# Order of a Strassen unit's products and of one closing product; deferred multiplications; later residual loads in an RWKV block with a feed-forward layer

## The chip, the cores and the metric

The kernel runs on one NeuronCore of a Trainium2 chip. The time is the device time of one execution in microseconds (us); of the kernel before there are three runs, and their median is the number that counts. The profile of a further execution gives the time of every instruction. Engines are named PE (TensorE matmuls), PEld (TensorE weight loads), DVE (VectorE), ACT (ScalarE), POOL (GpSimd) and SP (SyncE, which here only issues DMAs). PE, DVE and ACT each run their instructions in the order in which the program wrote them; they meet through semaphores. The order of the DMA issues on SP and POOL is set by the tile scheduler from the same program.

## The reference

The input is 2048 tokens of width 512 in float32. First comes an RWKV block on the normalised input, then a gated feed-forward layer:

```
y0 = layer_norm(x);  h = layer_norm(y0);  hh = time_shift(h)
k, v, r = (h*tm + hh*(1-tm)) @ W.T          (three mixes, three weights)
y  = y0 + sigmoid(r) * wkv(k, v) @ Wo.T
h  = layer_norm(y);  hh = time_shift(h)
kk = (h*cm_mk + hh*(1-cm_mk)) @ Wkey.T        (512 to 2048)
y  = y + sigmoid((h*cm_mr + hh*(1-cm_mr)) @ Wcr.T) * (silu(kk) @ Wval.T)
x  = x + y
z  = layer_norm(x)
out = x + (silu(z @ gate.T) * (z @ up.T)) @ down.T    (512 to 2048 to 512)
```

The wkv step needs only elementwise work per token. Nearly all the time is in the matrix products.

## The kernel before

**Blocks.** The tokens are worked off in four blocks of 512 (b = 0 to 3). The RWKV part of all blocks comes first, then the feed-forward part (FFN) of each block: for g = 0 to 3 a gate unit and an up unit (each 512 x 512 weights), then the down projection.

**A unit.** Each 512 x 512 x 512 product is split into quarters of 256 and done with Winograd's form of Strassen's scheme: seven products of quarters instead of eight. A1, A2, ... are quarters of the weights, B1, ... of the activations, S1 to S4 and T1 to T4 their sums. `unit` (L662 to L751) writes the seven products as steps. A product of quarters is 8 matmul records of 128x256. The steps share PSUM banks: an own bank z, and the two banks `accv` and `accx` that all units have in common.

- step 1 (A11 B11) fills z; ACT copies z to accv (L701).
- step 2 (A12 B21) adds on accv, which is then the output quarter (0,0) and goes to `sink`.
- step 6 (S2 T2) adds on z; ACT copies z to an SBUF tile u2 (L712).
- step 5 (S1 T1) adds on z; ACT copies z to accx (L716). DVE's `u2 -= accx` is put off by one product with `later` (L717).
- step 7 (S3 T3) adds on z: output quarter (1,1).
- step 3 (S4 B22) adds on accx: output quarter (0,1).
- step 4 (A22 T4) adds on z; DVE adds u2, which is output quarter (1,0).

Steps 7, 3 and 4 are not done at once: they go into the list `held`, and the next unit does them one at a time between its own steps (`pop_held`). So the common banks pass from one unit to the next while both are under way. The order of a unit of one weight is in L748; about 35 of 41 units find three held steps of a unit before them.

**Deferred work.** `later(fn, n)` puts a function on one list, `put_off`; each product calls `due()`, which counts the entries down and runs those that are due from the front of the list, in order. `tick` runs background work (mixes, norms, sums of weights) as far as a planner's estimate of DVE's time allows.

**Paired units.** In the FFN of blocks 1 to 3 the products A11 B11 and S3 T3 of a unit are themselves split once more (`inner`, L772 to L855); `paired_unit` (L859 to L946) works on banks accz, accw, accv and accx and adds the inner results (`pair`). Copies L930 and L931 bring an inner result into PSUM banks. Sinks of a gate unit apply Silu; those of an up unit multiply by the gate's result and write the hidden activations.

**Down projection.** `down_product` (L1615 to L1769) has seven outer products, each again split in seven on quarter-size tiles of 128x128 (one[0] to one[6]); z steps (0, 2, 4, 5, 6) add on one bank, and ACT copies it out after most of them (L1696); y steps (1, 3) add on another bank. `quads` are sums of the hidden activations.

**Loads.** Weights come through a ring of 12 tiles, issued by SP. `load_resid` (L1396) issues, on SP, one 1 MB load of the residual and four x loads of 256 KB; `paced` ties each to the end of the last product written before it. `ffn_in` adds them, takes the norm and transposes it into the next block's activations.

Of the kernel before, what the change touches and what calls it, by code (L numbers as in the profile page):

```python
# [64 lines left out]
def rwkv_ffn_kernel(  # L65
# [584 lines left out]
    held = []  # L650
# [11 lines left out]
    def unit(weights, Bs, sink, by_token, done=None, free=None):  # L662


        acc, tmp = {}, {}
        last = len(weights) - 1

        def product(z, a, b, first=False, between=None, part=None, read=None):
            if first:
                acc[z] = bank()  # L670
            pz = acc[z]
            groups = list(range(last + 1) if part is None else part)
            for g in groups:
                wg = weight(weights[g], a)
                act = Bs[g][b]
                for m in range(2):
                    for k in range(2):
                        lo = slice(m * P, (m + 1) * P)
                        lhsT = act[:, k, lo] if by_token else wg[:, k, lo]
                        rhs = wg[:, k, :] if by_token else act[:, k, :]  # L680
                        mm = nc.tensor.matmul(  # L681
                            pz[:, m, :],
                            lhsT=lhsT,
                            rhs=rhs,
                            start=first and g == 0 and m == 0 and k == 0,
                            stop=g == last and k == 1,
                            skip_group_check=True,
                        )
                latest[:] = [mm.ins.name]
                if read is not None and g == groups[-1]:  # L690
                    read()
                due()
                if g < groups[-1]:
                    tick()
                    if between is not None and g < 2:
                        between()

        def step1():
            acc["v"], acc["x"] = accv, accx
            product(  # L700
                "z", A11, B11, True, pop_held, read=lambda: nc.scalar.copy(accv, acc["z"])  # L701
            )

        def step2(part=None):
            product("v", A12, B21, part=part)
            if part is None or last in part:
                sink(0, 0, accv)

        def step6():
            product("z", S2, T2)  # L710
            tmp["u2"] = u_tile("u2")
            nc.scalar.copy(tmp["u2"], acc["z"])  # L712

        def step5():
            product("z", S1, T1)
            nc.scalar.copy(accx, acc["z"])  # L716
            later(lambda: tt(tmp["u2"], tmp["u2"], accx, ALU.subtract), 1)  # L717

        def step7():
            product("z", S3, T3)  # L720
            sink(1, 1, acc["z"])

        def step3():
            product("x", S4, B22)
            sink(0, 1, accx)

        def step4():
            product("z", A22, T4)
            tt(tmp["u2"], acc["z"], tmp["u2"], ALU.add)

            later(lambda: sink(1, 0, tmp["u2"]), 1)
            if free is not None:
                free()
            if done is not None:
                later(done, 2)
            quiet[0] = True

        if last > 0:

            def most():  # L740
                step2(range(last))

            def rest():
                step2([last])

            order = (step1, None, most, step6, rest, step5)
        else:
            order = (step1, None, step2, step6, None, step5, None)  # L748
        for s in order:
            if s is None:  # L750
                pop_held()  # L751
            else:
                s()
                tick()
        held.extend(((STEP, step7), (STEP, step3), (STEP, step4)))
# [103 lines left out]
    def paired_unit(at, b, n, after, sink, done=None, free=None):  # L859


        B = Lazy((b, "z"))
        st, steps = ahead.pop(at, (None, ()))
        for f in steps:
            f()
        steps = []
        if after is not None:
            ahead[after[0]] = inner(after[2], after[1])
            steps = ahead[after[0]][1]

        def small():
            if steps:
                steps.pop(0)()

        def product(dst, q, k, start=False):
            wg = weight(n, q)
            act = B[k]
            for m in range(2):
                for kk in range(2):
                    mm = nc.tensor.matmul(  # L880
                        dst[:, m, :],
                        lhsT=wg[:, kk, m * P : (m + 1) * P],
                        rhs=act[:, kk, :],
                        start=start and m == 0 and kk == 0,
                        stop=kk == 1,
                        skip_group_check=True,
                    )
            latest[:] = [mm.ins.name]
            due()

        z, aw = acc2["z"], acc2["w"]
        plus = None if st is None else st["r"][:, 1]
        u2 = None
        small()
        pop_held()
        if st is None:
            product(z, A11, B11, True)
            nc.scalar.copy(accv, z)
            tick()
            pop_held()  # L900
        small()
        product(z, S2, T2)
        if st is None:
            u2 = u_tile("u2")
            nc.scalar.copy(u2, z)
        else:
            nc.scalar.copy(aw, z)
        tick()
        pop_held()
        small()  # L910
        product(accv, A12, B21)
        sink(0, 0, accv)
        tick()
        if st is None:
            plus = bank()
            product(plus, S3, T3, True)
            tt(u2, plus, u2, ALU.add)
            plus7 = u_tile("p7")
            nc.scalar.copy(plus7, plus)
            plus = plus7  # L920
            tick()
        small()
        product(z, S1, T1)
        nc.scalar.copy(accx, z)
        sink(1, 1, z, plus)
        tick()
        small()
        if after is not None:
            r = ahead[after[0]][0]["r"][:, 0]
            nc.scalar.copy(z, r)  # L930
            nc.scalar.copy(accv, r)  # L931
        product(aw, A22, T4, st is None)
        end = sink(1, 0, aw, plus if u2 is None else u2)
        if end is not None:
            later(end, 1)
        tick()

        def last():
            product(accx, S4, B22)
            sink(0, 1, accx)  # L940
            if free is not None:
                free()
            if done is not None:
                later(done, 1)

        held.append((STEP, last))  # L946
# [509 lines left out]
    def ffn_gate(b, g):  # L1456
# [4 lines left out]
        def sink(i, j, c, plus=None):  # L1461
            t = tile_of("s")
            s[i, j] = t
            if plus is not None:
                tt(t, c, plus, ALU.add)
                c = t
                if (i, j) == (1, 0):
                    return lambda: nc.scalar.activation(t, t, AF.Silu)
            nc.scalar.activation(t, c, AF.Silu)

        if b == 0:
# [21 lines left out]
    def ffn_up(b, g):  # L1493
# [3 lines left out]
        def sink(i, j, c, plus=None):  # L1497
# [1 line left out]
            if q not in hid:  # L1499
                hid[q] = hidden_tile()  # L1500
            h = hid[q][:, g]
            if plus is not None:
                tt(h, c, plus, ALU.add)
                c = h
            tt(h, c, s[i, j], ALU.mult)
            if g == 3:
                made.add((b, q))
                if q in (B11, B22):
                    quarter_sums(b, 0 if q == B11 else 1)

        done = lambda: hidden_done(b, g)
        free = op_done if g == 3 else None
# [99 lines left out]
                parts.append(("T3", B22, B12))  # L1612
            urgent((b, "quarters", n, 1), run(parts))

    def down_product(b, sink, weight_of, final, done=None):  # L1615
        base = {}

        def summed(n, r):
# [49 lines left out]
        def steps(n):  # L1668
# [46 lines left out]
            def fifth():  # L1715
                product(st["z"], S1, T1, False)
                keep(0, 1)
                if n + 2 < 7:
                    later(lambda: quarter_sums(b, n + 2, (0,)), 1)
                later(rest, 1)  # L1720

            def rest():
                r = st["r"]
# [24 lines left out]
        for n in range(7):  # L1748
# [4 lines left out]
            one[0]()  # L1753
            tick(half)
            pop_held()
            one[1]()
            tick(half)
            if final and n == 6:
# [15 lines left out]
    def ffn_down(b):  # L1774
# [16 lines left out]
                store(1, cols)  # L1791
                store(0, slice(HB, HB + P))

        down_product(b, sink, down_weight, final)

# [81 lines left out]
    for b in range(NB):  # L1879
        for g in range(4):  # L1880
# [2 lines left out]
                ffn_gate(b, g)  # L1883
            if g == 1 and b == 0:
                push((b + 1, "z", "t"), ffn_in(b + 1), op_free)
            if g == 0 and 0 < b < NB - 1:
                load_resid(b + 1)
            ffn_up(b, g)
            if g == 0 and b == 0:
                load_resid(b + 1)  # L1890
            if g == 0 and 0 < b < NB - 1:
                push((b + 1, "z", "t"), ffn_in(b + 1), op_free)
        if b + 1 < NB:
            need((b + 1, "z"))
            ffn_gate(b + 1, 0)
# [83 lines left out]
```

## Time and profile before

| What | Value |
|---|---|
| Runs | 1229.54, 1229.62, 1232.41 us; median 1229.62 |
| Profiled execution | 1232.75 us, span from first to last instruction 1231.0 us |
| Mean granted TensorE clock | 0.998 |
| PE busy | 1216.0 us |
| DVE busy | 819.9 us |
| ACT busy | 408.1 us |
| POOL busy | 214.3 us |
| DMA | 321.98 MB, mean 262 GB/s |

A line of the timeline has the start in us, the duration, the engine, the line of the kernel, the operation, output <- inputs and the shape; the brackets at the end hold the engine's idle time before it and what ended it. In a list of waits the three numbers behind the colon are the total in us, the number of waits, and the longest. A wait of PE is written as what PE was about to do, an arrow, and the engine, tile and line that it waited for. A matmul group on the timeline that shows a wait also pays some 0.2 us until matmuls follow each other at the usual pitch of 0.22 us (128x256) or 0.11 us (128x128), so costs of stalls are best read from starts.

### The profile page before, as it was taken

How to read it: one execution, taken by the hardware profiler on the slowest of the kernel's cores; microseconds unless marked ns; L12 is line 12 of the kernel's file. 1: busy time of each engine (PE TensorE's matmuls, PEld its weight loads, DVE VectorE, ACT ScalarE, POOL GpSimd, SP SyncE). 2: the span in 40 equal slices, each digit the busy share in tenths (PEclk: the TensorE clock that was granted, in tenths of full speed). 3: DMA queues.
4: the chain of work that ended last, by engine and by line, in shares of the span. 5: the costliest groups of instructions: out<-in, count | busy, mean ns of one | idle time of the engine just before them, and what ended most of it. 6: DMA issues, size and time to landing. Idle time of an engine off the chain costs nothing.

```text
span 1231.0 us, 20030 instructions
## 1 busy us (share of the span) xinstructions
PE 1216.0 (99%) x7124; PEld 1106.3 (90%) x7124; DVE 819.9 (67%) x1530; ACT 408.1 (33%) x824; POOL 214.3 (17%) x386
## 2 busy tenths in 40 slices
PE   8999999999999999999999999999999999999998
PEld 7888888888888888998899888999999899999998
DVE  5886676677586667885867776557556575565466
ACT  5534252352532334313312222124431243323321
POOL 1332221223222223002205651000000000000000
PEclk9999999999999999999999999999999999999999
DMA  5768996799888989899889864896669856796576
GB/s 179 258 221 281 304 300 229 272 331 294 285 261 274 310 280 308 252 296 379 269 269 331 289 223 145 268 334 188 201 217 298 313 185 204 247 302 225 181 255 205
DMA packets 161978, 321.98 MB, mean 262 GB/s; under 512 B 19272, under 2 KB 32728, under 8 KB 160600
## 3 DMA queue, kind: packets, MB, share of 16 engines
q1 hardware_dynamic: 135312, 236.25, 59.5%
q0 software_dynamic: 24960, 81.81, 18.4%
q10 hardware_dynamic: 1608, 2.65, 0.6%
q8 instruction: 57, 0.93, 0.3%
q14 instruction: 41, 0.34, 0.1%
HBM read 267.15 MB, written 53.49 MB: 260 GB/s over the span
## 4 chain that ended last, share of the span: by engine, by line
PE 84%; DMA 6%; DVE 5%; ACT 2%; issue 2%; POOL 1%; ACTq 0%; POOLq 0%; DVEq 0%; SPq 0%
PE ps L681 26%; PE ps L1684 21%; PE accz L880 6%; PE accx L681 5%; PE accv L681 5%; PE ps L797 5%; PE ps L974 5%; PE accv L880 3%; PE accx L880 3%; PE accw L880 3%; PE ps L566 1%; DMA raw<-d 1%; DMA raw<-in_w 1%; DMA dd<-raw 1%; DMA raw<-in_wd 1%
## 5 line engine op out<-in xcount | busy, mean ns | idle before, releaser
L681 PE MATMUL ps<-mix,w 128*128 128x256 f32 x920 | 211.2, 379 | 1.7 <-ACT u L712 1.7
L681 PEld LDWEIGHTS ps<-mix,w 128*128 128x128 f32 x920 | 173.9, 190 | 25.6 <-ACT u L712 2.1
L1684 PE MATMUL ps<-w,hid 128*128 128x128 f32 x1248 | 156.9, 275 | 0.4 <-ACT r L1696 0.4
L1684 PEld LDWEIGHTS ps<-w,hid 128*128 128x128 f32 x1248 | 149.3, 192 | 1.4 <-ACT r L1696 0.5
L1684 PE MATMUL ps<-w,quads 128*128 128x128 f32 x1056 | 133.7, 275 | 0.9 <-ACT r L1696 0.7
L1684 PEld LDWEIGHTS ps<-w,quads 128*128 128x128 f32 x1056 | 126.1, 192 | 1.8 <-ACT r L1696 1.4
L1696 ACT COPY r<-ps 128x128 f32<-128x128 f32 x168 | 44.5, 266 | 205.6 <-PE ps L1684 202.4
L510 DVE TENSOR_TENSOR raw<-raw 128x512 f32<-128x512 f32 x92 | 63.3, 688 | 41.9 <-issue 18.6
L880 PE MATMUL accz<-zT,w 128*128 128x256 f32 x376 | 89.0, 380 | 0.0
L510 DVE TENSOR_TENSOR hid<-hid 128x512 f32<-128x512 f32 x126 | 86.2, 698 | 2.3
L880 PEld LDWEIGHTS accz<-zT,w 128*128 128x128 f32 x376 | 68.0, 190 | 7.4
L974 PE MATMUL ps<-mix,w 128*128 128x256 f32 x320 | 72.4, 386 | 1.1 <-DVE mix L518 1.1
L1780 POOL DMA_DIRECT2D out<-resid x12 | 8.6, 718 | 356.6 <-DVE resid L510 331.0
L974 PEld LDWEIGHTS ps<-mix,w 128*128 128x128 f32 x320 | 61.4, 194 | 10.2 <-DVE mix L518 1.8
L510 DVE TENSOR_TENSOR r<-ps,r 128x256 f32<-128x256 f32 x83 | 29.8, 359 | 57.9 <-PE ps L1684 53.6
L510 DVE TENSOR_TENSOR r<-r 128x128 f32<-128x128 f32 (+1 forms) x83 | 41.1, 496 | 36.3 <-ACT r L1696 34.9
L681 PE MATMUL ps<-w,t 128*128 128x256 f32 x264 | 59.4, 379 | 0.0
L510 DVE TENSOR_TENSOR quads<-hid,quads 128x512 f32<-128x512 f32 x84 | 57.7, 687 | 1.4
L797 PEld LDWEIGHTS ps<-inner,w 128*128 128x128 f32 x352 | 52.6, 191 | 6.2 <-ACT pair L808 1.5
L701 ACT COPY accv<-ps 128x512 f32<-128x512 f32 x41 | 23.4, 571 | 100.4 <-PE ps L681 97.6
L681 PEld LDWEIGHTS ps<-w,t 128*128 128x128 f32 x264 | 50.1, 190 | 6.8
L681 PE MATMUL ps<-zT,w 128*128 128x256 f32 x248 | 56.0, 379 | 0.0
(228 smaller groups left out, 2167.5 us busy)
## 6 DMA issues: line engine op xcount, KB each, us to landing
w<-in_w SPq DMA_DIRECT2D x237, 256.0 KB, 4.2
w<-sum SPq DMA_DIRECT2D x220, 256.0 KB, 4.1
w<-dd SPq DMA_DIRECT2D x112, 256.0 KB, 3.6
w<-vsum SPq DMA_DIRECT2D x56, 256.0 KB, 4.4
w<-vv SPq DMA_DIRECT2D x56, 256.0 KB, 3.9
w<-d SPq DMA_DIRECT2D x48, 256.0 KB, 3.6
w<-in SPq DMA_DIRECT2D x44, 256.0 KB, 3.6
q<-in_w POOLq DMA_DIRECT2D x36, 256.0 KB, 6.7
```

The source lines that it names most:

```text
L510: nc.vector.tensor_tensor(out, a, b, op)
L566: nc.tensor.transpose(flat[:, t * P : (t + 1) * P], h[:, t, c * P : (c + 1) * P], ident)
L681: mm = nc.tensor.matmul(pz[:, m, :], lhsT=lhsT, rhs=rhs, start=first and g == 0 and m == 0 and k == 0, stop=g == last and k == 1, skip_gro ...
L701: "z", A11, B11, True, pop_held, read=lambda: nc.scalar.copy(accv, acc["z"])
L797: m = nc.tensor.matmul(dst[:, i, :], lhsT=wt(i, q), rhs=act(i, k), start=start and i == 0, stop=True, skip_group_check=True,)
L880: mm = nc.tensor.matmul(dst[:, m, :], lhsT=wg[:, kk, m * P : (m + 1) * P], rhs=act[:, kk, :], start=start and m == 0 and kk == 0, stop=kk ...
L974: mm = nc.tensor.matmul(acc[i, j][:, m, :], lhsT=act[:, k, lo] if by_token else wg[:, k, lo], rhs=wg[:, k, :] if by_token else act[:, k, : ...
L1684: mm = nc.tensor.matmul(dst, lhsT=x[k][:, g, :], rhs=wt[:, g, :], start=first and g == 0, stop=g == 3, skip_group_check=True,)
L1696: nc.scalar.copy(st["r"][:, m, n * P : (n + 1) * P], st["z"])
L1780: eng.dma_start(out_t[b][:, tokens, cols], rs[b][:, tokens, cols])
```

## The change

There are four parts.

1. In `unit`, where three steps are held from a unit before, the order of a one-weight unit is step 1, held 7, held 3, step 6, step 2, held 4, step 5 instead of step 1, held 7, step 2, step 6, held 3, step 5, held 4. 
2. In paired units the second operation of the (1,1) and (1,0) sinks (Silu for gate, the multiplication for up) is put off by one product. Before, this was so for the gate's (1,0) only.
3. In the last of the seven outer products of block 0's down projection (n = 6, `alone`) the steps go 0, 2, 4, 1, 5, 3, 6 in one piece, with none held for what follows, and `rest` (the sums of r) is put off by three products instead of one.
4. For blocks 1 and 2 `load_resid(b+1)` is put off by four products into `ffn_up(b, 0)`; `ffn_in(b+1)` is pushed ahead of `ffn_up(b, 1)` instead of behind `ffn_up(b, 0)`.

```diff
@@ unit
             order = (step1, None, step2, step6, None, step5, None)
+            if len(held) == 3:
+                order = (step1, None, None, step6, step2, None, step5)
@@ paired_unit
-        sink(1, 1, z, plus)
+        later(sink(1, 1, z, plus), 1)
...
-        end = sink(1, 0, aw, plus if u2 is None else u2)
-        if end is not None:
-            later(end, 1)
+        later(sink(1, 0, aw, plus if u2 is None else u2), 1)
@@ ffn_gate, sink
                 tt(t, c, plus, ALU.add)
-                c = t
-                if (i, j) == (1, 0):
-                    return lambda: nc.scalar.activation(t, t, AF.Silu)
+                return lambda: nc.scalar.activation(t, t, AF.Silu)
@@ ffn_up, sink
-            if plus is not None:
-                tt(h, c, plus, ALU.add)
-                c = h
-            tt(h, c, s[i, j], ALU.mult)
-            if g == 3:
-                made.add((b, q))
-                if q in (B11, B22):
-                    quarter_sums(b, 0 if q == B11 else 1)
+
+            def end():
+                tt(h, c if plus is None else h, s[i, j], ALU.mult)
+                if g == 3:
+                    made.add((b, q))
+                    if q in (B11, B22):
+                        quarter_sums(b, 0 if q == B11 else 1)
+
+            if plus is None:
+                return end()
+            tt(h, c, plus, ALU.add)
+            return end
@@ down_product
-                later(rest, 1)
+                later(rest, 3 if alone and n == 6 else 1)
...
             pop_held()
+            if alone and n == 6:
+                one[2]()
+                tick(half)
+                pop_held()
+                for k in (4, 1, 5, 3, 6):
+                    one[k]()
+                    tick(half)
+                continue
             one[1]()
@@ ffn_down
-        down_product(b, sink, down_weight, final)
+        down_product(b, sink, down_weight, final, alone=b == 0)
@@ FFN loop
+            if g == 1 and 0 < b < NB - 1:
+                push((b + 1, "z", "t"), ffn_in(b + 1), op_free)
             if g == 0 and 0 < b < NB - 1:
-                load_resid(b + 1)
+                later(lambda: load_resid(b + 1), 4)
             ffn_up(b, g)
...
-            if g == 0 and 0 < b < NB - 1:
-                push((b + 1, "z", "t"), ffn_in(b + 1), op_free)
```

## The prediction

> **What bounds the kernel now.** I read the page first (busy time, then the chain that ended last), then PE's waits, then the timeline around each wait that the change can reach.
>
> ```profile
> PE 1216.0 (99%) x7124; PEld 1106.3 (90%) x7124; DVE 819.9 (67%) x1530; ACT 408.1 (33%) x824; POOL 214.3 (17%) x386
> ...
> PE 84%; DMA 6%; DVE 5%; ACT 2%; issue 2%; POOL 1%; ACTq 0%; POOLq 0%; DVEq 0%; SPq 0%
> ```
>
> PE is never idle for long, so time changes only where PE's waits come or go. The change adds and removes no matmul. PE's waits, with us in total, times and longest:
>
> ```profile
> PE ps L681 <- ACT u L712: 1.7, 1, 1.7
> PE accx L880 <- DMA w<-sum: 1.4, 1, 1.4
> ...
> PE ps L1684 <- ACT r L1696: 1.1, 3, 0.4
> ...
> PE accv L681 <- ACT accv L701: 0.9, 1, 0.9
> ...
> PE ps L797 <- ACT pair L808: 0.7, 2, 0.4
> ```
>
> These are all that the change can take away. By starts of successive matmuls, slow restart included, they cost 1.94 (at 426.67), 1.63 (973.32), 1.25 (813.71 and 815.22), 1.17 (321.10) and 1.24 (906.09 and 1048.41): 7.2 us.
>
> **1. The order in `unit` (about 35 of 41 units).** One product of 8 matmuls is 1.73 us. Before: s1, s7', s2, s6, s3', s5, s4' (a prime is a held step of the unit before). After: s1, s7', s3', s6, s2, s4', s5. ACT's copies get more room: accv's copy to s2 has three products instead of one, u2's copy to s5 two instead of one. So the 1.17 us at 321.10, a wait for the copy of accv, goes. What gets less room is s5's end: s5 copies its bank to accx, DVE then does `u2 -= accx`, and only then may s3 write accx. Before, five products lay between s5 and s3; now two do, 3.46 us. In the trace of before this DVE operation has enough room:
>
> ```profile
> L716 ACT COPY accx<-ps x41: 570/570/580, 109.0 to 764.5; 128x512 f32<-128x512 f32 x41
> ...
> DVE u L510: 28.1, 17
> ```
>
> The copy ends 0.55 to 0.76 us after s5. The subtraction ends 1.3 to 3.1 us after s5 in most units, which still fits, but +4.06 (at 109), +4.04 (214), +5.30 (315), +5.57 (415), +6.36 (583) and +5.37 (595) in six. With unchanged lags these six would stall 0.7 + 0.7 + 2.0 + 2.2 + 3.0 + 2.0 = 10.6 us against the 3.3 us that are free: one end. The other end is no stall at all and both old ones gone: -3.1. DVE's own order changes too, so I follow it unit by unit in the order of instructions that the change produces.
>
> The worst place is the r unit behind a k unit (blocks 2 and 3). The deferred list is served in order, and the k unit's last operation, due two products later, stands ahead of `u2 -= accx`; so DVE meets it only when s3 is next. This is what DVE does there in before:
>
> ```profile
> 254.91 0.69 DVE L518 SCALAR_TENSOR_TENSOR e<-e,r 128x512 f32<-128x512 f32 x1 [0.76 <-ACT r L1246]
> 255.51 0.68 DVE L510 TENSOR_TENSOR u<-u,accx 128x512 f32<-128x512 f32 x1
> 256.12 0.69 DVE L510 TENSOR_TENSOR u<-ps,u 128x512 f32<-128x512 f32 x1
> 256.73 0.68 DVE L510 TENSOR_TENSOR raw<-raw 128x512 f32<-128x512 f32 x1
> 257.33 0.61 DVE L514 TENSOR_SCALAR r<-u,nfirst 128x256 f32<-128x256 f32 x2
> 260.27 1.42 DVE L518 SCALAR_TENSOR_TENSOR mix<-hT_b,vec,mix 128x512 f32<-128x512 f32 x2 [2.33 <-ACT mix L619]
> 261.98 0.75 DVE L518 SCALAR_TENSOR_TENSOR mix<-hT_b,vec,mix 128x512 f32<-128x512 f32 x1 [0.29 <-ACT mix L619]
> ```
>
> The reader sees the subtraction at 255.51, ahead of the mix operations that wait for ACT. In after it is behind them. With the end of k's s4 as zero: u add to 0.9 and tensor_scalar to 1.5 (DVE), two Exp to 2.85, accx copy to 3.4, two mix activations to 4.7, accv copy to 5.3, one mix to 5.9 (ACT); DVE's third mix waits for that and ends at 6.7, the product with e at 7.4, the subtraction at 8.1. PE does s5 to 1.73, s1 to 3.46, s7 to 5.2, and s3 then waits until 8.2: 3.0 us. In block 3 the same chain holds, with raw loads that held DVE from 413.82 to 418.01 in before: 3.0 if they are in time, 6.0 if as late as then; I take 4.3, nearer to the first since the wait is shared, less the 1.94 us of 426.67 which these later copies replace: +2.4. At the value units near 585, with another raw load ahead, I take +1.2 (0 to 4). The other units keep 0.1 to 1.8 us of room. Sum 3.0 + 2.4 + 1.2 - 1.17 = **+5.4** (-3.1 to +10.6).
>
> A stall of this length would be new for this kernel; its longest in mid-run is 1.94 us, and the granted clock stays 0.998. The Trainium skill, "TensorE: Matmul & The Clock Gate", section "What's actually happening", says that TensorE drops to half clock after at least one idle window of about 3.4 us and needs another such window of work to come back. By that rule each of up to four new stalls could cost 1.7 us more (an estimate from that page), and the sum would be some 7 us higher. No row here has an idle time that long, and the sum goes without it.
>
> **2. Residual loads behind a unit's first weights (blocks 1 and 2).** `load_resid(b+1)` issues 1 MB of resid and four x loads of 256 KB. It is paced on a product that is now four products later, in the up unit's first product round. On SP these five go ahead of the S2 weight of the next gate unit; that weight stands behind them in the same queue. What this queue did at the place in before:
>
> ```profile
> 959.24 0.33 SPq L1398 DMA_DIRECT2D resid<-res  x1
> 959.78 2.65 SPq L310 DMA_DIRECT2D x<-in_x  x4
> 962.78 0.33 SPq L206 DMA_DIRECT2D w<-sum  x1
> 963.93 1.14 SPq L256 DMA_DIRECT2D w<-in  x2
> 967.31 1.00 SPq L206 DMA_DIRECT2D w<-sum  x2
> ```
>
> ```profile
> 973.32 1.53 PE L880 MATMUL accx<-zT,w 128*128 128x256 f32 x6 [1.40 <-DMA w<-sum]
> ```
>
> The weight issued at 967.31 had waited on the residual's landing and came 1.63 us late at 973.32. That stall goes. What is late next is the S2 weight. Between the pace point and the S2 product that reads it PE has 0.43 + 1.73 + 0.43 + 1.73 + 0.86 + 1.73 + 0.43 = 7.34 us of work. In block 1 of before resid was issued at 816.41, the weight behind x at 819.45, and it landed at 827.15: 10.7 us after resid's issue, itself 0.2 behind its pace point: 10.9, so 3.6 us too late. In block 2 the two weights issued next (963.93) landed 12.6 us after resid's issue, the one ahead of them (962.78) some 1.2 us earlier: 11.4, 4.1 too late. Together 7.7 less 1.63: **+6.1**. Lower bound: weights alone land 4.1 us after issue, which with 3.3 us of issue ahead is 7.4, no stall, hence -1.6. Upper: 5 us each, +8.4. I take the value near the top because the megabytes ahead are the same and move on the same queue. SP's later issues shift with it; POOL issues none of the moved loads. The adds and statistics of the next `ffn_in`, pushed one unit later, have DVE's idle third and a whole unit as cover; without it they would delay transposes, some 0.7 us each.
>
> **3. The closing product of block 0's down projection.** Two z steps in a row wait for ACT's copy of r:
>
> ```profile
> 813.71 1.16 PE L1684 MATMUL ps<-w,hid 128*128 128x128 f32 x8 [0.35 <-ACT r L1696]
> 815.22 1.05 PE L1684 MATMUL ps<-w,quads 128*128 128x128 f32 x7 [0.35 <-ACT r L1696]
> ```
>
> The new order 0, 2, 4, 1, 5, 3, 6 puts a y step between them, and the sums go to the end: -1.25. The first inner product then waits for the product's last addition, one DVE operation of 0.36 us of which about 0.2 shows: **-1.05** (-1.25 to +0.4).
>
> **4. Multiplications put off by a product in paired units.** The pair addition that ACT's copies L930 and L931 wait for came at 904.12, behind a 0.69 us multiplication. With this moved behind it, the addition starts up to 0.7 earlier, but its own product ends near 903.8. Two stalls of 0.62 shrink: **-0.8** (-1.24 to +0.3, if a gate's Silu, later by 1.7 us, holds up its multiplication).
>
> **Sum:** 5.4 + 6.1 - 1.05 - 0.8 = +9.6. The profiled execution took 1232.75 us (span 1231.0), 0.25% over the median of the runs, 1229.62. So 1242.4 for such an execution and 1239.2 on the median.
>
> **The rivals.** 0.3% (3.7 us) is what a measurement of this kernel can tell from no change.
> - *The room that is left suffices (faster).* The old stalls go, and what is late in my working arrives in time: `u2 -= accx` within 3.3 us of s5, the S2 weight within 7.34 us of the pace. For it: most lags are under 3.1 us, and a weight alone lands in 4.1. Against it: mix operations ahead of the subtraction, megabytes ahead of the weight. It gives -7.2 + 0.2: 1222.6. It decides as long as all new stalls together stay under 7.2 - 3.7 = 3.5 us; one late S2 weight uses that up.
> - *The load stalls come, the units are neutral.* If DVE's work in the r units is done earlier than I place it: 0 + 6.1 - 1.85 = +4.3: 1233.9.
> - *The unit stalls come, the loads don't.* 5.4 - 1.6 - 1.85 = +2: 1231.6, not distinguishable.
> - *Raw loads hold DVE in more units.* With the 10.6 end of part 1 and 5 us for each load: 10.6 + 8.4 - 1.85 = +17: 1246.8.
> - *Nothing visible.* The prolonged stalls are used up by others downstream: PE has no slack to give back, so this needs all terms small: 1229.6.
>
> **How the numbers follow.** My forecast 0.50; loads only 0.16 (slower, barely); raw loads 0.10; units only 0.09 and nothing 0.03 (same); all gains 0.12 (faster). Faster 0.12, same 0.13 with a little of the second case, slower 0.75. The range from 1228 to 1245 leaves out most of the gains case and half of the worst one. The likeliest case alone has 1235 to 1244.
>
> **What would show it.** In the changed profile PE's waits hold no ACT r L1696 pair and no accv L701; new entries are a wait of s3 (accx) for DVE u of about 3 us near 258 and again near 425, and two of the S2 product (accz) for DMA w<-sum of 3 to 4 us near 827 and 970. The prediction is wrong if the S2 weight overtakes the residual, if DVE reaches the subtraction before the mix operations, or if the clock falls behind a long stall.

## The result and the profile after

The changed kernel takes 1242.08 us (median of six runs, 1240.33 to 1244.87); the kernel before took 1231.06 us in its six. The ratio is 1.0091 with a 95% interval of 1.0073 to 1.0109, some 11 us slower. The profiled execution has a span of 1243.1 us, 12.1 more than before. It was also the longest of the six runs, so single sizes below are those of one execution.

The first line is the busy time on the page of the changed kernel; the others are PE's waits (us in total, times, longest).

```profile
PE 1221.1 (98%) x7124; PEld 1109.4 (89%) x7124; DVE 819.6 (66%) x1530; ACT 411.3 (33%) x824; POOL 214.9 (17%) x386
```

```profile
PE accz L882 <- DMA w<-sum: 4.6, 2, 3.1
PE accx L681 <- DVE u L510: 4.0, 3, 2.4
PE ps L681 <- ACT accx L716: 3.5, 3, 2.1
...
PE ps L1686 <- ACT r L1698: 0.4, 1, 0.4
```

The reader sees the exchange: all five old entries (ACT u, DMA w<-sum at accx, the pairs of ACT r and ACT pair, ACT accv) are gone, and three new ones have come. They are the three resources that the change gave less room: the S2 weight, `u2 -= accx`, and the copy to accx. PE's busy time rose by 5.1 us although it does the same 7124 matmuls; that is explained below.

By starts of matmuls (time over the usual pitch, restart included) the whole difference can be placed:

| Place in the changed kernel | before | after |
|---|---|---|
| 113, s3 waits for DVE u | 0.8 | 2.0 |
| 172.6, s7 waits for ACT accx | 0 | 0.7 |
| 222, transposes wait for DVE h | 0.3 | 1.25 |
| 264.65, s3 waits for DVE u | 0 | 2.7 |
| 321, s2 waits for ACT accv | 1.2 | 0 |
| 424 to 429 | 1.9 | 4.95 |
| 488.6, s7 waits for ACT accx | 0 | 1.2 |
| 515, 596, 763 | 1.1 | 0.3 |
| 813 to 827, closing product and after it | 1.7 | 0.7 |
| 841.8, S2 weight, block 1 | 0 | 1.8 |
| 985.3, S2 weight, block 2 | 0 | 6.1 |
| old late weight (973) | 1.6 | 0 |
| pairs (906, 1048) | 1.2 | 0 |

The differences add up to 11.9 of the 12.1 us: +7.8 up to 763 (the units, the transposes near 222 and the small waits at 515, 596 and 763), loads +6.3, closing product -1.0, pairs -1.2. Of the 2.0 at 113, 0.85 stands before and after alike, near 108.

The place behind the k unit, DVE's timeline of the changed kernel, answers to the lines shown of before:

```profile
258.32 0.69 DVE L510 TENSOR_TENSOR raw<-raw 128x512 f32<-128x512 f32 x1
260.90 1.42 DVE L518 SCALAR_TENSOR_TENSOR mix<-hT_b,vec,mix 128x512 f32<-128x512 f32 x2 [1.89 <-ACT mix L619]
262.64 0.75 DVE L518 SCALAR_TENSOR_TENSOR mix<-hT_b,vec,mix 128x512 f32<-128x512 f32 x1 [0.33 <-ACT mix L619]
263.31 0.69 DVE L518 SCALAR_TENSOR_TENSOR e<-e,r 128x512 f32<-128x512 f32 x1
263.92 0.68 DVE L510 TENSOR_TENSOR u<-u,accx 128x512 f32<-128x512 f32 x1
```

PE's timeline there:

```profile
255.13 7.13 PE L681 MATMUL ps<-mix,w 128*128 128x256 f32 x32
264.65 1.56 PE L681 MATMUL accx<-mix,w 128*128 128x256 f32 x6 [2.39 <-DVE u L510]
```

The subtraction now stands behind three mix operations, which wait for ACT (1.89 and 0.33 us), and behind the product with e, and s3 waits for it.

SP's timeline in block 2, then PE's:

```profile
974.82 0.32 SPq L1398 DMA_DIRECT2D resid<-res  x1
975.36 2.25 SPq L310 DMA_DIRECT2D x<-in_x  x4
977.65 0.44 SPq L206 DMA_DIRECT2D w<-sum  x1
```

```profile
981.59 0.61 PE L799 MATMUL ps<-inner,w 128*128 128x128 f32 x4
985.29 1.65 PE L882 MATMUL accz<-zT,w 128*128 128x256 f32 x3 [3.09 <-DMA w<-sum]
```

The weight is issued 2.8 us behind the residual load and is there 7.6 us later; in block 1 it was issued at 835.63 and the S2 product started at 841.83, 6.2 us later.

**A second cost behind the longest waits.** After two of the waits PE ran at half clock. The view of busy time in stretches gives the granted clock (PEclk, the column behind the engines):

```profile
424.36:427.00 2.64, 2.64 (x6) 2.09 (x7) 1.68 (x3) 2.64 (x5) 1.72 (x4) 0.52 0.94 313
985.00:988.50 3.50, 3.21 (x8) 2.58 (x9) 0.27 (x1) 0.00 (x0) 0.00 (x0) 0.50 0.74 274
264.00:268.00 4.00, 3.35 (x16) 2.96 (x17) 2.55 (x5) 0.60 (x1) 0.00 (x0) 1.00 0.14 36
```

Behind the wait at 424.36 (2.07 us idle) 7 matmuls of 256 columns came at 0.43 us instead of 0.22. Behind the one at 985.29 (3.09 idle) 17 matmuls came at twice their pitch, 9 of 256 columns at 0.43 and 8 of 128 columns at 0.21 instead of 0.11. By starts this costs 1.4 and 2.8 us beyond the waits. Behind the 2.39 us at 264.65 nothing of the kind happened; the last section shows why. These 4.2 us are in the table and are most of what PE's busy time gained.

### The profile page after: what moved, and what is told of

It is laid out like the page before. It is cut to its first block, busy times and chain, and to the rows that moved or that the text cites. A ratio compares the mean times of both kernels' runs of the same rounds, so it can differ in the third digit from the quotient of the medians.

```text
span 1243.1 us, 20067 instructions
## 1 busy us (share of the span) xinstructions
PE 1221.1 (98%) x7124; PEld 1109.4 (89%) x7124; DVE 819.6 (66%) x1530; ACT 411.3 (33%) x824; POOL 214.9 (17%) x386
## 3 DMA queue, kind: packets, MB, share of 16 engines
q10 hardware_dynamic: 1608, 2.65, 0.6%
## 4 chain that ended last, share of the span: by engine, by line
PE 88%; DVE 4%; DMA 3%; ACT 2%; issue 1%; SPq 0%; POOL 0%; ACTq 0%; DVEq 0%
PE ps L681 28%; PE ps L1686 21%; PE accz L882 6%; PE accx L681 6%; PE accv L681 6%; PE ps L799 5%; PE ps L974 5%; PE accv L882 3%; PE accx L882 3%; PE accw L882 3%; PE ps L566 1%; DMA w<-sum 1%; DMA raw<-in_w 1%; ACT mix L619 1%; DMA row<-stats 1%
## 5 line engine op out<-in xcount | busy, mean ns | idle before, releaser
L510 DVE TENSOR_TENSOR raw<-raw 128x512 f32<-128x512 f32 x92 | 63.1, 686 | 27.4 <-issue 11.4
L510 DVE TENSOR_TENSOR u<-ps,u 128x512 f32<-128x512 f32 x42 | 28.9, 689 | 56.6 <-PE ps L681 56.6
L712 ACT COPY u<-ps 128x512 f32<-128x512 f32 x41 | 24.0, 584 | 109.2 <-PE ps L681 109.2
```

The source lines that it names most:

```text
L510: nc.vector.tensor_tensor(out, a, b, op)
```

## The experiments

**The four parts alone.** Each kernel is the one before with one part of the diff, here in short.

```diff
e1_units:  + if len(held) == 3:
           +     order = (step1, None, None, step6, step2, None, step5)
e2_loads:  - load_resid(b + 1)        + later(lambda: load_resid(b + 1), 4)
           ffn_in pushed before ffn_up(b, 1) instead of behind ffn_up(b, 0)
e3_close:  + for k in (4, 1, 5, 3, 6): ...   later(rest, 3 if alone and n == 6 else 1)
e4_pairs:  + later(sink(1, 1, z, plus), 1)   later(sink(1, 0, aw, ...), 1)
```

> Only the order in unit is changed. Theory (DVE's subtraction and ACT's copy of accx come too late in a few units): the waits seen up to 765 us in the changed kernel come back at the same places, s3 for DVE u near 113, 264.7 and 429, s7 for ACT accx near 172.6, 424.4 and 488.6, and the one at 321 is gone. By starts of matmuls these are worth about +7.8 us, some 1.4 of it at half clock behind the stall at 424. Time 1.0055 to 1.007 of before. Rival (the slower half of the kernel is the FFN, units are neutral): within 0.2% of before, and the stalls at 264 and 424 hang on another part of the change.

> Only the later residual loads, with ffn_in pushed one unit later. Theory (the S2 weight stands behind 2 MB on SP's queue): a wait of accz for DMA w<-sum of about 1.5 us in block 1 and about 3 us in block 2, the second followed by some 2.5 us at half clock, and no wait at the old place of 1.63 us: +6 us, 1.004 to 1.006 of before. Rival (the stalls come from the deferred multiplications holding up DVE and with it the ring): no DMA wait of more than 1 us at S2, time within 0.2% of before.

> Only the closing product of block 0's down projection. Theory: the two waits of PE for ACT r near 814 go, 1.25 us, and 0.2 us of waiting for the product's last addition comes: -1.05 us, 0.999 of before. Rival (the next inner product waits for r in place of them): no change in time and a wait of L799 for DVE or ACT of 1 us right behind.

> Only the deferred second operations of paired units. Theory: the two waits of PE for ACT pair, 0.62 us each near 906 and 1048, go, since the pair addition no longer stands behind a multiplication: -1.2 us, 0.999 of before. Rival (the waits went because the other parts shifted DVE's work): both waits are still there, time unchanged.

| Kernel | median us | before us | ratio, 95% interval | us against before |
|---|---|---|---|---|
| e1_units | 1241.40 | 1231.21 | 1.0084 (1.0066 to 1.0103) | +10.3 |
| e2_loads | 1235.72 | 1231.21 | 1.0034 (1.0022 to 1.0045) | +4.2 |
| e3_close | 1229.78 | 1231.21 | 0.9984 (0.9972 to 0.9995) | -2.0 |
| e4_pairs | 1228.93 | 1231.21 | 0.9977 (0.9967 to 0.9987) | -2.8 |

The last column is the ratio less one, times 1231.2. The four add to +9.7 against +11.2 for all together, within the intervals: the parts hardly touch each other as far as these intervals tell, and the first is nearly the whole loss. PE's waits of e1_units, then of e2_loads:

```profile
PE accx L681 <- DVE u L510: 5.7, 3, 2.4
PE ps L681 <- ACT accx L716: 1.8, 1, 1.8
```

```profile
PE accz L880 <- DMA w<-sum: 3.7, 2, 2.5
```

In e1_units the waits at 113, 262, 423 and 427 come back with nothing else changed; those near 172 and 488 are 0.2 and nothing, so they depend on the execution. By starts this profile, of the fastest of its six runs, shows +7.0 of the +10.3 (behind the first 20 us). The rival that the units are neutral is out. In e2_loads both S2 weights are late without any deferred multiplication, so that rival is out too; the late weight of before is gone. No half clock followed its 2.49 us, so that the profile shows +3.0 us by starts (behind the first 20 us); of the +4.2 of the runs the rest is not placed. In e3_close the two waits near 814 went and 0.5 us of other short waits stayed behind them, -1.25 by starts. In e4_pairs both waits for ACT pair went, and with them two of 0.24 us (0.40 by starts) near 858 and 1000 where transposes waited for ACT zT. These two stand again in the changed kernel, near 878 and 1025, so they are not owed to this part alone, and what else made the 2.8 is not placed.

**What holds the subtraction back.** Two kernels put `u2 -= accx` elsewhere in the changed kernel: at once behind the copy, or still put off by one product but at the front of the deferred list.

```diff
-            later(lambda: tt(tmp["u2"], tmp["u2"], accx, ALU.subtract), 1)
+            tt(tmp["u2"], tmp["u2"], accx, ALU.subtract)                                   # e5_sub_now
+            put_off.appendleft([0, lambda: tt(tmp["u2"], tmp["u2"], accx, ALU.subtract)])  # e11_front
```

> The changed kernel, but u2 -= accx is written right behind ACT's copy in step 5 instead of being put off by one product. Theory (the subtraction stands behind mix operations and deferred work on DVE): s3's waits for DVE u near 113, 264.7 and 429, 4.9 us by starts, go or shrink under 0.5 us each; s7's waits for ACT accx (near 172, 424 and 488, 3.9 us and the half clock behind them) stay, since ACT's own queue is not changed. Time 3 to 5 us below the changed kernel, so about 1.005 of before. Rival (the copy on ACT is what is late, DVE only passes it on): the waits stay at the same places with the same length, and DVE waits for ACT instead.

> The changed kernel with one difference: u2 -= accx, still put off by one product, goes to the front of the deferred list, so that the k unit's entry (due two products later) no longer holds it back. On DVE this moves it ahead of the last mix and the product with e in two places, the r units near 264 and 428. Theory (the list served in order holds the subtraction back there): the waits of accx for DVE u at these two places (2.65 us and 1.2 to 2.6 us by starts) go, since the subtraction needs only the copy of accx; the one near 113 and the waits for ACT accx stay. 3 to 5 us below the changed kernel. Rival (whatever is in front, the subtraction comes too late because ACT's copy or DVE's earlier mix operations are late): the two waits shrink by under 1 us.

e5_sub_now took 1242.48 us, 1.0089 of before (1.0075 to 1.0102): no gain at all over the change. All waits for DVE u are gone, also the one near 113, so at these places the rival (ACT's copy is what is late) is out. But a new wait of 3.31 us came, with 2.7 us lost at half clock behind it. ACT's, DVE's and PE's timelines show it:

```profile
104.83 2.54 ACT L619 ACTIVATE mix<-hT_b,onem 128x512 f32<-128x512 f32 x4
107.28 0.58 ACT L716 COPY accx<-ps 128x512 f32<-128x512 f32 x1
```

```profile
107.89 0.69 DVE L510 TENSOR_TENSOR u<-u,accx 128x512 f32<-128x512 f32 x1 [2.23 <-ACT accx L716]
108.49 2.73 DVE L518 SCALAR_TENSOR_TENSOR mix<-hT_b,vec,mix 128x512 f32<-128x512 f32 x4
```

```profile
109.34 2.04 PE L681 MATMUL ps<-w,mix 128*128 128x256 f32 x4 [3.31 <-issue]
```

DVE stands still for 2.23 us on the copy, which ACT does behind four mix activations, and the mix operations that the next product reads are now behind it. The profile names no releaser for PE's wait; a quarter of the 2.73 us puts the end of the first mix at 109.2 (an estimate), just ahead of PE's start. The expectation of 3 to 5 us gained was wrong: written too early, the subtraction blocks DVE's queue just as the mix operations blocked it when it was written too late.

e11_front moves the subtraction on DVE ahead of the mix operations in the r units; between 271 and 291 and near 436 DVE's order differs too. It took 1238.93 us, 1.0060 (1.0042 to 1.0079), 3 to 4 below the changed kernel. DVE's timeline at the first place:

```profile
258.63 0.69 DVE L510 TENSOR_TENSOR u<-u,accx 128x512 f32<-128x512 f32 x1 [1.24 <-ACT accx L716]
259.28 1.42 DVE L518 SCALAR_TENSOR_TENSOR mix<-hT_b,vec,mix 128x512 f32<-128x512 f32 x2
```

s3 starts at 260.48 with no wait, and the wait of the second place is gone as well. So the entry of the k unit in the list, served in order, was what held the subtraction back there. What stays: 1.6 us came up at 274, where DVE stood idle for 2.9 us in front of `raw` operations that are ahead of the next unit's subtraction, and ACT's late copy to accx made 2.77 us of waiting near 422, with half clock behind it and behind the 2.57 us for the S2 weight at 980.

**What makes the S2 weight late.** Two kernels send loads of the changed kernel through POOL's queue: both, or x alone.

```diff
-        paced(nc.sync.dma_start(r, resid[b]))
-        loads[b] = r, load_x(b)
+        eng = nc.gpsimd if 1 < b < NB else nc.sync
+        paced(eng.dma_start(r, resid[b]))
+        loads[b] = r, load_x(b, (eng,) * NT)                                   # e6_pool_queue
+        loads[b] = r, load_x(b, (nc.gpsimd,) * NT if 1 < b < NB else None)     # e12_x_pool, resid on SP
```

> The changed kernel, but the residual and x loads of blocks 2 and 3 are issued by POOL instead of SP, at the same point of the program with the same pace. Theory (the S2 weight is late because it stands behind the loads on SP's queue: their pace, their issue and their bytes): the S2 weight is issued when the ring has room, and the waits for DMA w<-sum (1.76 and 3.25 us, and 2.5 us of half clock) go or fall under 1 us each; 4 to 7 us below the changed kernel, 1.004 of before. Rival (2 MB on the same 16 DMA engines is what delays it, on whatever queue): each wait stays within 1 us of what it was.

> The changed kernel, but only the four x loads of blocks 2 and 3 go to POOL; the residual's 1 MB load stays on SP ahead of the S2 weight, with its pace. Theory (issue time and bytes ahead in the queue add up): the weight is issued 2.3 us earlier and has 1 MB ahead instead of 2: the waits for DMA w<-sum go in block 1 and fall to 1 us or less in block 2. Rival (the pace of the residual load, behind which the weight waits, or the 1 MB load alone makes it late): waits within 0.7 us of 1.2 to 1.8 in block 1 and 2.7 to 3.3 in block 2.

e6_pool_queue: 1237.60 us, 1.0052 (1.0036 to 1.0067), 4.5 below the changed kernel. There is no wait for DMA w<-sum at all. SP's and POOL's timelines in block 2:

```profile
971.36 0.55 POOL L1399 DMA_DIRECT2D resid<-res  x1
971.90 2.14 POOL L310 DMA_DIRECT2D x<-in_x  x4
```

```profile
971.09 0.32 SPq L206 DMA_DIRECT2D w<-sum  x1
971.50 0.38 SPq L206 DMA_DIRECT2D w<-in_w  x1
971.98 0.45 SPq L206 DMA_DIRECT2D w<-sum  x1
```

The S2 weight is the load at 971.09: SP issues the same 833 loads in the same order in both kernels, and the S2 weight is the same one of them. It no longer has to wait until the paced residual and the x loads are out; it goes 0.27 us ahead of the residual, 7.2 us before its product starts at 978.30, where the changed kernel issued it 4.6 us before PE was ready for it. In block 1 it goes 0.53 us ahead (830.98 against 831.51) and lands 2.6 us later. So its place behind the loads on SP's queue is what made it late.

The rival (the bytes on the engines, on whatever queue) is not out, though, for no late weight stood behind the bytes here. The next w<-sum, issued at 971.98, 0.6 us behind POOL's residual, took 8.1 us to land, in block 1 6.9: as long as the S2 weight took behind the loads on its own queue, against a median of 4.1 for such loads in the kernel before. They were needed later and made no wait. e12_x_pool, 1237.05 us (1.0048, 1.0029 to 1.0066), agrees: the wait in block 1 is gone, the one in block 2 is 1.24 us where 1 or less was expected. With 1 MB instead of 2 ahead on SP, and x going out on POOL in the same microseconds, the weight, issued at 973.02, 0.37 behind the residual instead of 2.8, still took 8.2 us. Issue time and bytes both count, and the bytes do so from the other queue as well; how they divide these runs do not settle.

**Versions that beat the kernel before.** The parts that help (closing product, deferred multiplications) with the old order of units, and the loads of blocks 2 and 3 cut in eight:

```diff
     def due():
+        if trickle:
+            trickle.popleft()()
...
+        for k in range(NT):
+            part(r[:, k, :], resid[b][:, k, :])     # trickle.append(lambda: paced(nc.sync.dma_start(...)))
+            part(t[:, k, :], x_t[b][:, k, :])
...
-                load_resid(b + 1)
+                spread_resid(b + 1)
```

> The kernel before with the closing product and the deferred multiplications of the change, the old order of the units, and the residual and x loads of blocks 2 and 3 cut into eight loads of 256 KB, one behind each of eight products. Theory (a burst of 2 MB ahead of one weight is what makes it late): no wait for DMA w<-sum over 0.5 us in either block, neither the old one at 973 nor the S2 ones: -1.2 -1.0 -1.6 us and a little more, as those parts gave 2.0 and 2.9 when alone: 0.995 to 0.997 of before. Rival (the ring has no room for 2 MB at any place of the unit): one or more weights are late by 1 us or more in each block, 0.998 or above.

e8_spread: 1227.31 us, 0.9975 (0.9962 to 0.9987), a little less gained than expected; short waits of 0.8 us near 164 to 170 and 1.0 us at 219 stand in its profile that before had at 0.3 together. No wait for a weight is left in either block: between the pieces, weights in block 2 landed 4.5 to 6 us after their issue. That a burst ahead of one weight makes it late is so shown from the other side.

```diff
+            if len(held) == 3:
+                order = (step1, None, step6, step2, None, step5, None)
```

> As the one with spread loads, and in units behind three held steps the two own steps 2 and 6 are swapped: s1, s7', s6, s2, s3', s5, s4'. This leaves five products between s5 and s3 and gives the copy u2 two products instead of one before s5. Theory (room in front of s3 is what the change lost; the swap keeps it): the wait for ACT u near 425 (1.4 to 1.9 us) goes and no wait of s3 for DVE u or of s7 for ACT accx comes: 1.5 us below the one with spread loads. Rival (any change of the order opens a new wait elsewhere: s6 now comes one product behind the copy to accv): new waits of L681 for ACT accv of 1 us or more in several units, time not below the one with spread loads.

e9_swap: 1229.05 us, 0.9987 (0.9978 to 0.9997), not below e8_spread, so the theory missed. The rival had the time right, but no waits of 1 us for ACT accv came, only 0.6 us in place of the old one at 321. A new wait of 1.53 us came at 111.52 instead, for which the profile names no releaser; DVE's mix operation behind the subtraction ends there at 111.4. And the wait for ACT u near 426 stayed, 1.67 us. ACT's timeline tells why:

```profile
418.01 0.57 ACT L705 COPY accv<-ps 128x512 f32<-128x512 f32 x1 [2.49 <-PE ps L685]
421.81 0.63 ACT L1249 ACTIVATE e<-r 128x512 f32<-128x512 f32 x1 [3.23 <-DVE r L518]
...
425.94 0.56 ACT L716 COPY u<-ps 128x512 f32<-128x512 f32 x1
```

ACT stands for 3.23 us in front of an Exp whose input DVE delivers late, and the copy stays behind this Exp wherever PE's product is. More products between two steps help nothing when the copy's place on ACT is behind other work.

```diff
+        units[0] += 1          # counts calls of unit
...
+            if units[0] == 15:
+                order = (step1, None, None, step6, step2, None, step5)
```

> The kernel with spread loads, closing product and deferred multiplications, old order of the units, and the changed order in one unit alone, the one whose step 2 waits for ACT's copy to accv near 321. Theory (the new order gives that copy two products more, and this unit's s3 and s7 have room): that wait, 0.9 to 1.1 us by starts, goes and no other comes; 1 us below the kernel with spread loads, 0.9965 of before. Rival (the wait moves to the held steps of the next unit): the same time as with spread loads, and a new wait of s3 or s7 near 325 to 335.

e10_one_unit: 1225.02 us, 0.9949 (0.9934 to 0.9965), the fastest, 17 us below the changed kernel. The wait near 321 is gone and did not move on. The wait near 425 shrank to 0.3 as well, which was not expected: DVE's idle time in front of `raw` operations near 413 was 2.1 us instead of 4.1 in e8_spread, so that the Exp and the copy behind it on ACT came earlier. That the planner, asked at other moments, wrote the loads of `raw` elsewhere is likely, but not shown. How much of the gain over e8_spread is owed to the one and how much to the other is not separated. The longest of PE's waits that are left:

```profile
PE ps L470 <- POOL ident masks.py:199: 1.4, 1, 1.4
PE ps L980 <- DVE mix L522: 1.1, 1, 1.1
PE ps L570 <- ACT zT L1439: 0.5, 2, 0.2
PE ps L570 <- DVE z L518: 0.4, 1, 0.4
```

The first two are the start of the kernel.

## Why the prediction was right, and where not

The forecast of 1239.2 us, slower, was right: 1242.08, inside both ranges; +9.6 was forecast, +11.2 measured. The two causes that it named, the subtraction and the S2 weight, are the ones that the runs show. That the sum came so near is partly luck: alone the parts gave +10.3, +4.2, -2.0 and -2.8 where +5.4, +6.1, -1.05 and -0.8 stood, and these errors add up to nearly nothing.

**Part 1 (+5.4; placed at +7.8 in the profile, +10.3 when alone).** The chain in the r unit came as worked out, and by order: subtraction behind three mixes and the product with e, 2.65 us at 264.65 where 3.0 was forecast. e11_front shows the cause that was named, the deferred list served in order. Near 425 the estimate was 4.3; it was 4.95, but made of two waits (copy to accx 2.3, subtraction 1.2) and 1.4 at half clock. Two terms failed. The 1.2 us near 585 did not come. And "the other units keep 0.1 to 1.8 us of room" did not hold in three: 1.1 us near 113, where the lag row had already said 0.7 and the hand working overruled it, and 0.7 and 1.2 us near 172 and 488, where not DVE's subtraction but ACT's copy to accx is late for s7. That step went from two products behind s5 to one; the prediction worked out only s3's condition and passed over s7's. These two vary with the execution (nothing at 488 in e1_units), as room of 0.1 us does. In sum, the terms that were worked out (264, 425, 585 and 321) came to +4.5 instead of +5.4, and 1.4 of that is half clock; +3.3 came from places that stood at nothing: the waits near 113, 172 and 488, the transposes near 222 (+0.95, cause open), less small waits that went.

**Part 2 (+6.1; +6.3 in the profile, +4.2 when alone).** That the S2 weight is late because it stands behind the loads on SP's queue is shown by e6_pool_queue, where it went ahead of them; the forecast took the megabytes as moving on that queue, and e6_pool_queue shows that they slow the weights issued behind them from another queue as well. The sizes were too high: 1.8 instead of 3.6 in block 1 and 3.35 instead of 4.1 in block 2. PE's work up to the S2 product was about right (7.4 us from the residual's issue, where 7.34 from the pace point was counted); the weight landed 8.8 and 10.4 us behind the residual's issue instead of 10.7 and 11.4, and the issue of x took 2.2 instead of 2.6. (The two weights of 963.93 before, from which the 11.4 was taken, landed 12.8 and 13.3 us behind the residual, not 12.6.) The half clock behind the second made up for it, so that the sum was right for one part by an error and an omission of like size.

**Parts 3 and 4 (-1.05 and -0.8; -1.0 and -1.2 in the profile).** Right; both pairs of waits went. Alone they gave 2.0 and 2.8, each with an interval of some 1.3 us to both sides. What stood directly ahead of the pair addition at 904.12 was a sum of `quads`; the multiplication that the change moves stood one operation further ahead, at 902.79.

**The clock.** The prediction told a rule of the Trainium skill ("TensorE: Matmul & The Clock Gate", "What's actually happening") in sentences apart and kept it out of the sum, as no row of before had such an idle time. The forecast also named a fall of the clock behind a long stall as a sign that it would be wrong, and that sign came. It should have been weighed in: 4.2 of the 12.1 us are half clock. Without them the profile's sum would have been 7.9, below the forecast.

**The rivals.** "The room that is left suffices" fell at both of its conditions. "Loads only" is what e2_loads alone would be; the units were far from neutral. Of the fourth rival, DVE held by raw loads at many s3 steps, the runs show at most the one place at 274 in e11_front, beside the one near 418 that the forecast counted itself (DVE idle for 2.98 us there in the changed kernel).

## What to carry to other kernels

When a buffer that two stages share is released by a chain of engines (here PE's product, ACT's copy, DVE's subtraction), count the room of every later writer, the product after next and the next one alike, and find the releasing operation's place in its engine's queue: what stands in front of it decides, not its length. A load of megabytes belongs where no late weight stands behind it; another queue lets the weight go ahead, but what is issued behind the load is as slow there (e6_pool_queue). Cut in pieces and put between weights, it left no wait for a weight (e8_spread). Moving an order in all of a kernel's units for the sake of a wait in one of them cost 10 us; in that unit alone (e10_one_unit) the wait went and none came in its place.

## What the runs showed of the hardware

The half clock after PE's idle times was not expected at these lengths. Over the profiles of the kernel before, the changed one and all experiments, after the first 20 us, PE had 17 idle times of 1.1 to 1.8 us, and matmuls behind them kept their pitch of 0.22 us. Of 17 idle times of 2.07 to 3.31 us, 8 were followed by some 6 to 17 matmuls at twice their pitch (0.43 us for 256 columns), which cost some 1.4 to 2.8 us on top. The same wait of 2.39 us was followed by it in e1_units (at 261.86) and not in the changed kernel (at 264.65).

The traces show what decides. The pace changes only at points of a grid with a step of 3.413 us. In e11_front it first doubles at 6.92, halves at 423.35, doubles at 426.76 and again at 983.14: 122, 123 and 286 steps behind the first. All 10 changes that can be timed behind the first 20 us, in five profiles, lie within 0.01 us of a whole number of steps from the first change of their execution. That first change falls between 4.5 and 7.2 us, at another time in each execution, so the grid does not start with the kernel. Laid on these grids, the 8 waits with half clock behind them each put 2.07 to 2.44 us of idle time into one step; none of the 26 others put more than 1.91 us into any step. Busy time by steps in e1_units, where the wait of 2.39 us falls whole into the first step shown, and then in the changed kernel, where a point of the grid divides it (PEclk is the third number from the end):

```profile
259.15:262.56 3.41, 1.02 (x5) 0.65 (x4) 3.08 (x6) 1.77 (x4) 0.00 (x0) 1.00 0.56 159
262.56:265.98 3.42, 3.42 (x9) 2.72 (x9) 0.83 (x2) 0.60 (x1) 0.00 (x0) 0.50 0.00 0
265.98:269.39 3.41, 3.41 (x17) 2.98 (x17) 1.34 (x3) 0.59 (x1) 1.54 (x3) 1.00 0.54 153
...
260.64:264.05 3.41, 1.62 (x8) 1.09 (x6) 2.82 (x5) 3.06 (x6) 0.00 (x0) 1.00 0.75 234
264.05:267.47 3.42, 2.82 (x13) 2.51 (x14) 1.97 (x4) 0.60 (x1) 0.00 (x0) 1.00 0.08 30
```

The half clock starts with the step behind, as far as its start falls on running matmuls. In four of the eight cases it fell wholly on running matmuls and lasted one step, at a cost of 1.7 us; behind the two longest waits, which ran on into the next step, it lasted two. The Trainium skill ("TensorE: Matmul & The Clock Gate", "What's actually happening") names an idle window of about 3.4 us as the condition for half clock and calls the window free-running. The step and its free start agree with that; but a step with 2.07 us of idle time was enough here, and no idle time of this case fills a whole one.

Of the changed kernel's six runs, the three with a mean granted clock of 0.995 or 0.996 took 1243.3 to 1244.9 us and the three with 0.997 to 1.000 took 1240.3 to 1240.9, so a good part of their spread goes with the half clock.
